# Two graph layers on one Trainium2 core: layer 1's early part over 17 blocks instead of 18, with five late lists, and a reordered tail

## Chip, core, metric

The kernel runs on one core of one Trainium2 chip. The metric is device time in microseconds (us). The kernel before has a median of 489.83 us over 9 runs (489.35 to 491.16).

Engines: TensorE (PE in the profile; PEld is its weight load), VectorE (DVE), ScalarE (ACT), GpSimd (POOL), SyncE (SP). Each works through its own queue strictly in the order in which the program recorded the instructions. SP issues plain DMAs; POOL issues the indirect ones (a gather or a scatter of 128 rows of 2 KB by a list of row numbers).

## What is computed

Cut to what matters, N = 2708 rows, D = 512, everything float32:

```python
# layer 0
d   = rowsum(adj) ** -0.5
x   = layernorm(x + relu((d[:,None] * adj * d[None,:]) @ x @ W + b))
# layer 1, 4 heads
xn     = x @ W_node + b_node
feats  = einsum('nd,hdf->hnf', xn, K)
logits = s[:, :, None] - 1e10 * (1 - adj)      # attn = softmax(logits)
x   = layernorm(x + relu(mean_h(attn @ feats)))
```

`adj` is sparse: about 0.3% of its entries are nonzero, with values between 0.05 and 1, and the diagonal is always there. The factor -1e10 makes the softmax a choice: each row takes the one column with the largest entry of `adj`. So layer 1 is `u = h @ M + c` for every row (`M` is `W_node` times the mean of the four `K`), then `y[row] = u[idx[row]]`, then `layernorm(h + relu(y))`. A flag sends the kernel into a dense path where this would not hold; with these inputs that path is not taken.

## The kernel before, in words

**Blocks and chunks.** The 2708 rows are 22 blocks of 128 (the last has 20). A search stage finds up to seven nonzeros in each third of a row. Then the main loop (line 1146) runs over `NS` = 21 blocks, and in each over nine chunks c = 0 to 8. A chunk is one gather of 128 rows of `v = d * (x @ W)` by POOL (L611) and one addition of it: c = 0, 3, 6 by DVE (L662), the other six by two-pass matmuls of PE (L672). POOL fetches up to 22 chunks ahead, but the last eight chunks of a block need that block's list, which DVE makes two blocks earlier (`hot`, `listed`).

**Layer 0's norm and h @ M.** At c = 8 `norm_1` adds the block up (L711, L712), and ACT squares it (L721). In the next block come `root_1` (ACT square root, L742; one DVE operation, L743), `root_2` (four small DVE operations, L748 to L751), `nbs` (L1186) and `norm_3` (ACT, L756), which gives the block's rows `h`. SP stores them to `h_d`. PE then turns them (`turn_h`, L224), ACT copies the turned tile to `sT` (L226), PE multiplies by `M` (`u_product`, L235), DVE adds `c` (`u_store`, L790), and the result `u` goes to DRAM.

**The 22nd part, L.** Up to 128 rows with too many nonzeros are listed and computed as a dense row product over the loop (`acc_l`, L1012, until block 17). They are normed (L1022, L1023, L761), turned and multiplied as one more block, `L`.

**Early and late.** `u` is kept in two DRAM tensors: `u_e` holds the rows of the first `EARLY` = 18 blocks, `u_d` the rest. Once blocks 0 to 17 and `L` are in `u_e`, the rows whose `idx` points into `u_e` can be finished: `y_fetch(n)` gathers `u_e` by `idx` for block n (L1052), `y_1` adds and squares (DVE L1063 and L720, ACT L721), `root_1` and `root_2` do three blocks together, `y_3` norms (ACT L756, or DVE L761 for each third block), and SP stores the block to the output. Rows whose `idx` points into `u_d` are the late ones: they were ranked beforehand into `NLATE` = 4 lists of 128 rows. After the last block, `late_h` gathers their `h`, `fetch_some` their `u`, and `put` (L1029) scatters the finished rows over the output. The rows of `L` are a fifth such list.

**What orders the work.** The order is written out by hand in the loop. `later(k, f)` issues f k chunks on. The pieces of layer 1 are the list `early_y`, from which `pieces_y(1)` takes one; `y_ahead(k)` issues the next k fetches. In the kernel before, `u_product` of block b runs in block b + 2 for the last blocks (at c = 1; block 17 at block 18, c = 8), the first puts into `u_e` follow at blocks 18 and 19, and the pieces start four chunks after the puts become possible, three in four chunks. Three blocks of `y_1` are done when the loop ends, and the other 18 follow.

Of the kernel before, what the change touches and what calls it, by code (L numbers as in the profile page):

```python
# [39 lines left out]
F32 = mybir.dt.float32  # L40
# [10 lines left out]
NEG = -10000000000.0  # L51
GAP = -200.0
CAP = 128
EARLY = 18
NLATE = 4
DIRECT = 1
ROOTS_AT = 10
BY_VECTOR = range(1, 21)
# [5 lines left out]
def tile_two_graph_layers(  # L64
# [552 lines left out]
    def row_space():  # L617

        ring[0] += 1
        if late is not None and ring[0] % 2:  # L620
            return late.tile([P, D], F32, name="g2", bufs=12)
        return g_pool.tile([P, D], F32, name="g", bufs=12)

    def fetch_chunk(ib, c):
# [157 lines left out]
    def u_store(ib):  # L782

        pr = P if ib == L else rows(ib)
        ut = dl["u"] if ib == L else pool2.tile([P, D], F32, name="ut", bufs=2)
        po, on_pe = products_u.pop(ib)
        if on_pe:
            nc.scalar.copy(ut[:pr], po[:pr])
        else:
            nc.vector.tensor_add(ut[:pr], po[:pr], c_bc[:pr])  # L790
        if ib < EARLY - 1:
            store(u_e, ut, ib)
        elif ib == EARLY - 1:
            later(1, lambda: put(ut, u_e[:, :], dl["own"][:, ib : ib + 1], EARLY * P))
        elif ib != L:
            late_put = lambda: put(ut, u_d[:, :], dl["own_d"][:, ib : ib + 1], N - EARLY * P)
            late_put() if ib >= NS - 2 else later(3, late_put)
        u_done.add(ib)


# [257 lines left out]
            oob_is_err=False,  # L1058
        )

    def y_1(n):
        t = h_of[n]
        nc.vector.scalar_tensor_tensor(t, ys[n], 0.0, t, op0=ALU.max, op1=ALU.add, accum_out=tot[:, n : n + 1])  # L1063
        squares(n, P, t, ys.pop(n))


    def y_3(n):
        (norm_3 if n % 3 else norm_v)(n, P, h_of[n])


    GROUP = 3
    n_pieces = NS + 13
    early_y = [[] for _ in range(n_pieces)]
    for n in range(NS):
        last = n // GROUP * GROUP + GROUP - 1
        early_y[n].append(lambda n=n: y_fetch(n))
        early_y[n + 6].append(lambda n=n: y_1(n))
        if n == last:
            early_y[last + 8].append(lambda n=n: root_1(n - GROUP + 1, n + 1))
            early_y[last + 9].append(lambda n=n: root_2(n - GROUP + 1, n + 1))  # L1080
        early_y[last + 10 + n % GROUP].append(lambda n=n: (y_3(n), store(out, h_of[n], n)))

    def pieces_y(k):
        for _ in range(k):
# [61 lines left out]
    for ib in range(NS):  # L1146
        pr = rows(ib)
        for c in range(C):
            n = ib * C + c
            form_until(n + 11)  # L1150
            fetch_until(n + (9 if n < 14 else 11) + (0 if found_at is None else min(11, max(0, 2 * (ib - found_at - 3)))))
            add_chunk(ib, c)
            group_of = max(g for g in GROUPS if g <= hot_next)
            if (
                c in (0, 5)
                and hot_next < NS
                and hot_next <= ib + (2 if c == 0 else 4)
                and group_of in starts
                and not (c == 5 and found_at is not None and ib == found_at + 1)
            ):  # L1160
                hot(hot_next)
                listing[n + 4] = lambda k=hot_next: enlist(k)
                listing[n + 6] = lambda k=hot_next: listed(k)
                hot_next += 1
            if n in listing:
                listing.pop(n)()
            if ib == 0 and c in (5, 8):
                weights(2 if c == 5 else 3)
            if finds and c in ((1, 4, 7) if ib < 3 else (1, 5)):
                search_next()  # L1170
            if c == 2 and not finds and found_at is None:
                group(GROUPS[2])
                searching[0] = False
                found_at = ib
            if found_at is not None:
                for f in plan.pop((ib - found_at, c), []):
                    f()
            if c == 2 and ib > ROOTS_AT:
                root_1(ib - 1, ib)
            if c == (2 if ib <= ROOTS_AT else 3) and ib:  # L1180
                k = slice(ib - 1, ib)
                if ib <= ROOTS_AT:
                    norm_2(ib - 1, ib, rows(ib - 1))
                else:
                    root_2(ib - 1, ib)
                    nc.scalar.activation(nbs[:, k], nms[:, k], AF.Copy, scale=rss[:, k])  # L1186
                norm_3(ib - 1, rows(ib - 1), space(ib - 1))
                store(h_d, space(ib - 1), ib - 1)
                waiting_h.append(ib - 1)
            if c == (7 if ib < EARLY else 6):  # L1190
                for _ in range(2):
                    if waiting_h:
                        turn_h(waiting_h.pop(0))
            for k in sorted(products_u):
                u_store(k)
            if c == (5 if ib < EARLY else 8 if ib == EARLY else 1) or (ib == EARLY and c == 5):
                for k in sorted(hTs):
                    u_product(k)
            if found_at == ib - 3 and c == 4:
                products_l = list(range(NB))  # L1200
            if c % 2 and products_l:
                listed_turn(products_l.pop(0))
            elif len(dl.get("turned", [])) > (2 if products_l else 0):
                listed_product(dl["turned"].pop(0))
            if dl.get("at") == n - 2:
                root_1(L, L + 1)
                root_2(L, L + 1)
                norm_v(L, P, h_of[L])
                waiting_h.append(L)
            if L in h_of and "at" not in dl:  # L1210
                dl["at"] = n
            if "set" not in dl and u_done >= set(range(EARLY - 1)) | {L}:
                dl["set"] = n
                later(3, lambda: put(dl["u"], u_e[:, :], dl["put"][:, NLATE:], EARLY * P))
                later(5, lambda: put(dl["u"], u_d[:, :], dl["put_d"], N - EARLY * P))
            if "go" not in dl and u_done >= set(range(EARLY)) | {L}:
                dl["go"] = n + 4
            if n >= dl.get("go", n + 1) and (n - dl["go"]) % 4 != 3 and n < len(chunks) - 3:
                pieces_y(1)
            tick()  # L1220
        if not finds and late is None:

# [18 lines left out]
    assert not due and not products_u  # L1241

    ib = NS - 1
    u_product(ib - 1)
    y_ahead(4)
    u_store(ib - 1)
    root_1(ib, ib + 1)
    root_2(ib, ib + 1)
    norm_v(ib, P, space(ib))
    store(h_d, space(ib), ib)  # L1250
    stir(16)
    turn_h(ib)
    u_product(ib)
    y_ahead(4)
    pieces_y(5)
    for k in range(NLATE):
        late_h(k)
    u_store(ib)
    ys[L] = row_space()
    fetch_some(ys[L], dl["top"][:, NLATE:], u_e[:, :], EARLY * P)  # L1260
    y_ahead(NS)

    order = [L + 1, L + 2, L] + list(range(L + 3, L + 1 + NLATE))
    for n in order:
# [8 lines left out]
        k = NLATE if n == L else n - L - 1  # L1273
        put(h_of[n], out_views[k], dl["put"][:, k : k + 1])

    pieces_y(16)
    bad1 = small.tile([P, 1], F32, name="bad1")
    nc.vector.tensor_reduce(bad1, bad, axis=AX.X, op=ALU.max)
    po = p_po.tile([P, D], F32, name="po")
    nc.tensor.matmul(po[:1, :1], bad1, ones, start=True, stop=True)  # L1280
    for n in first:
        y_1(n)
        pieces_y(1)
    root_1(min(first), max(first) + 1)
    for n in second:
        y_1(n)
        pieces_y(1)
        if n == second[0]:
            root_2(min(first), max(first) + 1)
            for k in first:  # L1290
                y_3(k)
    root_1(second[0], second[-1] + 1)
    pieces_y(n_pieces)
    for n in first:
        rows_out(n)
    root_2(second[0], second[-1] + 1)
    nc.vector.tensor_copy(bad_i, po[:1, :1])
    for n in second:
        y_3(n)
        rows_out(n)  # L1300
    main.close()
    in_order.close()
# [144 lines left out]
```

## Time and profile before

| | |
|---|---|
| median of 9 runs | 489.83 us |
| the profiled execution | 491.44 us |
| its span, first to last instruction | 489.7 us |
| mean granted TensorE clock | 0.917 of full |
| busy share of the span | DVE 80%, PE 77%, ACT 64%, POOL 62% |
| `norm_1` of block 15, 16, 17, 18, 19, 20 starts (DVE L711) | 366.31, 379.44, 395.96, 406.47, 416.12, 428.73 us |
| first and last fetch of `u_e` by `idx` (POOL L1052) | 420.24, 458.28 us |
| first and last gather of late `u` from `u_d` | 459.75, 465.03 us |
| last scatter to the output, its issue ends | 483.46 us |

The page of the profile gives sums over the whole span. The change touches only the last quarter, so it is read by the timeline of each engine (start, duration, engine, line, operation, and in brackets the idle time before it with what ended it) and by a table of windows (busy time of each engine in a stretch, with the granted clock PEclk and the DMA share).

### The profile page before, as it was taken

The page shows a single profiled execution, that of the slowest core. Times are in us where ns is not written, and L with a number is a line of the kernel's source. Part 1 is how long each engine was busy: PE and PEld are TensorE (multiplying, and loading weights), DVE is VectorE, ACT ScalarE, POOL GpSimd, SP SyncE. Part 2 cuts the span into 40 slices and gives each one's busy share as a digit, 9 for nine tenths or more (in the row PEclk, how much of TensorE's full clock was granted, in tenths as well). Part 3 has the DMA queues.
Part 4 walks back from the last instruction along what each step waited for, and adds up shares of the span by engine and source line. Part 5 has one row for each costly group of instructions (what it writes and reads, how often), then busy time and mean ns, then how long its engine had stood idle before and what let it go on. Part 6 is the DMA issues. An engine that isn't in the chain of part 4 may idle for free.

```text
span 489.7 us, 5318 instructions
## 1 busy us (share of the span) xinstructions
PE 375.6 (77%) x1129; PEld 168.4 (34%) x1129; DVE 392.9 (80%) x1079; ACT 312.5 (64%) x575; POOL 305.9 (62%) x434
## 2 busy tenths in 40 slices
PE   5968787667988989799878858799999999782000
PEld 3434343333223333344323423344444444340000
DVE  2899979899499999999999995766666797548761
ACT  2599999797986556776772454855566322337880
POOL 2343544453477577777777676777777565677703
PEclk9999999998997989999989979799999999977555
DMA  7999999998548678889888789999999687468952
GB/s 225 420 398 414 422 336 372 362 327 331 197 124 288 189 232 270 258 260 311 280 247 292 224 271 385 360 331 380 345 374 301 213 272 255 138 186 274 329 212 84
DMA packets 51565, 140.67 MB, mean 287 GB/s; under 512 B 10617, under 2 KB 10617, under 8 KB 48688
## 3 DMA queue, kind: packets, MB, share of 16 engines
q0 software_dynamic: 21840, 68.29, 44.9%
q1 hardware_dynamic: 29684, 71.95, 39.0%
q8 instruction: 11, 0.18, 0.2%
q14 instruction: 30, 0.25, 0.1%
HBM read 117.33 MB, written 24.99 MB: 291 GB/s over the span
## 4 chain that ended last, share of the span: by engine, by line
DVE 29%; PE 28%; DMA 21%; ACT 9%; issue 9%; POOL 1%; SPq 1%; POOLq 0%; DVEq 0%; ACTq 0%
PE acc L672 12%; DMA a<-in_adj_dram 12%; PE po L235 8%; DMA x<-in_x_dram 5%; DVE ats L319 5%; DVE vals L318 4%; PE acc_l L1012 4%; DVE hot L393 2%; DMA l_a<-in_adj_dram,to_read 2%; DVE vs L662 2%; ACT a L305 2%; ACT a L299 2%; PE tp L224 1%; PE po L504 1%; DVE past L392 1%
## 5 line engine op out<-in xcount | busy, mean ns | idle before, releaser
L611 POOL DMA_INDIRECT g<-v_d,l_col x126 | 127.8, 1014 | 43.3 <-issue 23.1
L672 PE MATMUL acc<-g,s 128*128 128x512 f32 x278 | 144.4, 634 | 3.9 <-DMA g<-v_d,l_col 2.6
L235 PE MATMUL po<-m_sb,sT 128*128 128x512 f32 x176 | 83.8, 622 | 4.0 <-ACT sT L226 4.0
L235 PE MATMUL acc<-w_sb,sT 128*128 128x512 f32 (+1 forms) x176 | 82.4, 613 | 0.0
L611 POOL DMA_INDIRECT g<-v_d,cols x63 | 62.8, 997 | 19.7 <-issue 11.6
L318 DVE MAX8 vals<-a 128x8 f32<-128x896 f32 (+2 forms) x66 | 71.7, 1086 | 2.0 <-ACT a L299 2.0
L319 DVE FIND_INDEX8 ats<-vals,a 128x8 uint32<-128x896 f32 (+2 forms) x66 | 72.0, 1091 | 0.0
L672 PEld LDWEIGHTS acc<-g,s 128*128 128x128 f32 x278 | 50.1, 200 | 50.3 <-issue 43.0
L305 ACT ACTIVATE a<-a 128x2708 f32<-128x2708 f32 (+1 forms) x22 | 54.1, 2460 | 13.6 <-DVE ats L319 13.6
L299 ACT ACTIVATE a<-a 128x2708 f32<-128x2708 f32 (+1 forms) x22 | 54.4, 2473 | 10.5 <-POOL a L311 10.5
L235 PEld LDWEIGHTS po<-m_sb,sT 128*128 128x128 f32 x176 | 34.5, 200 | 47.7 <-issue 39.8
L649 ACT ACTIVATE s<-s,l_val,l_minus 128x128 f32<-128x128 f32 x86 | 42.4, 493 | 2.9
L235 PEld LDWEIGHTS acc<-w_sb,sT 128*128 128x128 f32 (+1 forms) x176 | 32.4, 195 | 34.1 <-issue 34.0
L226 ACT COPY sT<-tp 128x512 f32<-128x512 f32 (+1 forms) x44 | 25.4, 577 | 28.3 <-PE tp L224 28.3
L311 POOL TENSOR_SCALAR_AFFINE_SELECT a<-a 128x128 f32<-128x128 f32 (+1 forms) x22 | 6.6, 299 | 57.2 <-DMA a<-in_adj_dram 52.0
L224 PE MATMUL tp<-ident,x 128*128 128x128 f32 (+1 forms) x88 | 15.0, 298 | 30.8 <-DMA x<-in_x_dram 21.6
L662 DVE SCALAR_TENSOR_TENSOR vs<-g,scaled,vs 128x512 f32<-128x512 f32 x50 | 37.3, 745 | 0.1
L648 ACT ACTIVATE s<-place,l_row 128x128 f32<-128x128 f32 x86 | 33.4, 388 | 0.0
L393 DVE SCALAR_TENSOR_TENSOR hot<-slots,ends,past 128x256 bf16<-128x256 bf16 x63 | 30.6, 485 | 2.2
L1052 POOL DMA_INDIRECT g<-u_e,idx x21 | 22.2, 1058 | 7.9 <-issue 5.5
L224 PEld LDWEIGHTS tp<-ident,x 128*128 128x128 f32 (+1 forms) x88 | 10.3, 151 | 42.7 <-issue 25.0
L726 ACT ACTIVATE nms<-tot 128x1 f32<-128x1 f32 x10 | 2.0, 202 | 35.1 <-DVE h_early L712 20.1
(265 smaller groups left out, 579.0 us busy)
## 6 DMA issues: line engine op xcount, KB each, us to landing
a<-in_adj_dram SPq DMA_DIRECT2D x21, 1354.0 KB, 9.5
x<-in_x_dram SPq DMA_DIRECT2D x21, 256.0 KB, 19.3
vs<-v_d SPq DMA_DIRECT2D x21, 256.0 KB, 4.8
xr<-in_x_dram SPq DMA_DIRECT2D x21, 256.0 KB, 5.8
l_v<-v_d SPq DMA_DIRECT2D x21, 256.0 KB, 5.9
u_e<-ut SPq DMA_DIRECT2D x17, 256.0 KB
h_d<-h_late SPq DMA_DIRECT2D x13, 256.0 KB, 2.8
out_dram<-h_late SPq DMA_DIRECT2D x13, 256.0 KB, 4.3
```

The lines of the kernel that those rows point to most:

```text
L224: nc.tensor.transpose(ps[:, f, :pr], src[:pr, f * P : (f + 1) * P], ident[:pr, :pr])
L235: nc.tensor.matmul(po[:pr], sT[:, f, :pr], wt[:, f, :], start=(f == 0 and row_3 is None), stop=(f == ND - 1))
L299: nc.scalar.activation(a, a, AF.Copy, accum_out=sums[:pr, ib : ib + 1])
L305: nc.scalar.activation(a, a, AF.Relu, scale=-1.0, accum_out=bad[:pr, NB + ib : NB + ib + 1])
L318: nc.vector.max(out=vals[:pr, ib, t, :], in_=part)
L319: nc.vector.max_index(out=ats[:pr, ib, t, :], in_max=vals[:pr, ib, t, :], in_values=part)
L393: nc.vector.scalar_tensor_tensor(h_t[:, t, :], slots, ends[:, 0, ib - lo, t : t + 1], past, op0=ALU.is_gt, op1=ALU.subtract)
L611: nc.gpsimd.indirect_dma_start(out=t[:pr], out_offset=None, in_=src, in_offset=bass.IndirectOffsetOnAxis(ap=ap, axis=0))
L648: nc.scalar.activation(s[:, :pr], place[:, :pr], AF.Abs, bias=minus_row[:, t : t + 1])
L649: nc.scalar.activation(s[:, :pr], s[:, :pr], AF.Relu, scale=minus_val[:, t : t + 1], bias=val[:, t : t + 1])
L662: nc.vector.scalar_tensor_tensor(vs, g, scaled[:, ib, CHUNKS[c][1], 0:1], vs, op0=ALU.mult, op1=ALU.add)
L672: nc.tensor.matmul(acc[ib][:pr], ss.pop((ib, c))[:k, :pr], g[:k], start=(first and not bias_on_pe(ib)), stop=(c == len(CHUNKS) - 1),)
```

## The change

- `EARLY` is 17 and `NLATE` is 5. So `u_e` is complete one block sooner, one more list of late rows is gathered, fetched and put, and the lists' ranking on DVE has one more step per list.
- From block 16 on, `root_1` is at c = 1, `root_2` and `norm_3` at c = 2, `turn_h` at c = 5 and `u_product` at c = 3 or 7 of the **next** block: `u` of block b is made in block b + 1. The products of 14 and 15 are both in block 16, those of 16 and `L` in block 17, and 17, 18 and 19 in blocks 18, 19 and 20.
- The puts into `u_e` follow the products by one and two chunks, and from three chunks on one `y_fetch` is issued per chunk. In POOL's queue the three puts and the first fetch now stand ahead of the nine gathers of block 20, and two more fetches stand among these.
- From seven chunks after that point on, a piece of layer 1 is taken at c = 2, 5 and 8: additions 0 to 6 are in the loop (0 in block 18; 1, 2, 3 in 19; 4, 5, 6 in 20).
- `root_1` and `root_2` of layer 1 go over groups of 5, 5, 5, 3 and 3 blocks; all norms but two are ACT's.
- Row buffers: 12, 9 and 4 in a cycle of seven instead of 12 and 12.
- After the loop: fewer transposes that do nothing but keep PE busy (`stir`), the fetches are all issued, the norm of block 20 comes after one piece, and the late lists are done three and three.

```diff
-EARLY = 18
-NLATE = 4
+EARLY = 17
+NLATE = 5
...
-        if late is not None and ring[0] % 2:
-            return late.tile([P, D], F32, name="g2", bufs=12)
+        if late is not None and ring[0] % 7 % 2:
+            return late.tile([P, D], F32, name="g2", bufs=9)
+        if late is not None and ring[0] % 7 == 6:
+            return late.tile([P, D], F32, name="g3", bufs=4)
...
-            late_put() if ib >= NS - 2 else later(3, late_put)
+            late_put() if ib >= NS - 1 else later(1, late_put)
...
+    ENDS = [5, 10, 15, 18, NS]
+    early_y = [[] for _ in range(NS + 16)]
+    lo = 0
+    for hi in ENDS:
+        for n in range(lo, hi):
+            early_y[n].append(lambda n=n: (y_add(n), y_square(n)))
+        early_y[hi].append(lambda lo=lo, hi=hi: root_1(lo, hi))
+        early_y[hi + 1].append(lambda lo=lo, hi=hi: root_2(lo, hi))
+        for n in range(lo, hi):
+            out_n = lambda n=n: (y_3(n, n > 13 and n % 3 == 0), store(out, h_of[n], n))
+            early_y[hi + 2 + (n - lo)].append(out_n)
+        lo = hi
...
-            if c == 2 and ib > ROOTS_AT:
+            if c == (2 if ib < EARLY - 1 else 1) and ib > ROOTS_AT:
                 root_1(ib - 1, ib)
-            if c == (2 if ib <= ROOTS_AT else 3) and ib:
+            if c == (3 if ROOTS_AT < ib < EARLY - 1 else 2) and ib:
...
-            if c == (7 if ib < EARLY else 6):
+            if c == (7 if ib < EARLY - 1 else 5):
...
-            if c == (5 if ib < EARLY else 8 if ib == EARLY else 1) or (ib == EARLY and c == 5):
+            if c == 5 and ib < EARLY - 1 or ib >= EARLY - 1 and c in (3, 7):
                 for k in sorted(hTs):
                     u_product(k)
...
-                later(3, lambda: put(dl["u"], u_e[:, :], dl["put"][:, NLATE:], EARLY * P))
-                later(5, lambda: put(dl["u"], u_d[:, :], dl["put_d"], N - EARLY * P))
+                later(1, lambda: put(dl["u"], u_e[:, :], dl["put"][:, NLATE:], EARLY * P))
+                later(2, lambda: put(dl["u"], u_d[:, :], dl["put_d"], N - EARLY * P))
...
-                dl["go"] = n + 4
-            if n >= dl.get("go", n + 1) and (n - dl["go"]) % 4 != 3 and n < len(chunks) - 3:
-                pieces_y(1)
+                dl["go"] = n + 3
+            if n >= dl.get("go", n + 1):
+                y_ahead(1)
+                if n >= dl["go"] + 4 and c % 3 == 2:
+                    pieces_y(1)
...
-    u_product(ib - 1)
-    y_ahead(4)
-    u_store(ib - 1)
     root_1(ib, ib + 1)
+    pieces_y(1)
     root_2(ib, ib + 1)
     norm_v(ib, P, space(ib))
     store(h_d, space(ib), ib)
-    stir(16)
+    stir(12)
     turn_h(ib)
+    y_ahead(NS)
+    pieces_y(2)
     u_product(ib)
-    y_ahead(4)
-    pieces_y(5)
+    pieces_y(2)
     for k in range(NLATE):
         late_h(k)
-    u_store(ib)
...
+    u_store(ib)
```

More of the change, by code (lines that the diff above doesn't have):

```diff
@@ L1059, in fetch_some, with y_add, y_square, y_3 @@
         )
-    def y_1(n):
+    def y_add(n):
         t = h_of[n]
         nc.vector.scalar_tensor_tensor(t, ys[n], 0.0, t, op0=ALU.max, op1=ALU.add, accum_out=tot[:, n : n + 1])
[L1064 to L1081, printed above, removed]
+        nc.vector.tensor_scalar(nms[:, n : n + 1], tot[:, n : n + 1], -1.0 / D, None, op0=ALU.mult)
+    def y_square(n):
+        k = slice(n, n + 1)
+        nc.scalar.activation(ys.pop(n), h_of[n], AF.Square, bias=nms[:, k], accum_out=sqs[:, k])
+    def y_3(n, by_vector=False):
+        (norm_v if by_vector else norm_3)(n, P, h_of[n])
+    ENDS = [5, 10, 15, 18, NS]
[10 more added lines that the diff above has]
+        lo = hi
     def pieces_y(k):
@@ L1250, in tile_two_graph_layers @@
     store(h_d, space(ib), ib)
-    stir(16)
+    stir(12)
     turn_h(ib)
+    y_ahead(NS)
+    pieces_y(2)
     u_product(ib)
-    y_ahead(4)
-    pieces_y(5)
+    pieces_y(2)
     for k in range(NLATE):
         late_h(k)
-    u_store(ib)
     ys[L] = row_space()
     fetch_some(ys[L], dl["top"][:, NLATE:], u_e[:, :], EARLY * P)
-    y_ahead(NS)
+    u_store(ib)
     order = [L + 1, L + 2, L] + list(range(L + 3, L + 1 + NLATE))
@@ L1274, in rows_out @@
         put(h_of[n], out_views[k], dl["put"][:, k : k + 1])
-    pieces_y(16)
+    pieces_y(NS + 16)
     bad1 = small.tile([P, 1], F32, name="bad1")
@@ L1281, in tile_two_graph_layers @@
     for n in first:
-        y_1(n)
-        pieces_y(1)
+        y_add(n)
+        y_square(n)
     root_1(min(first), max(first) + 1)
     for n in second:
-        y_1(n)
-        pieces_y(1)
+        y_add(n)
+        y_square(n)
         if n == second[0]:
@@ L1291, in tile_two_graph_layers @@
                 y_3(k)
-    root_1(second[0], second[-1] + 1)
-    pieces_y(n_pieces)
     for n in first:
         rows_out(n)
+    root_1(second[0], second[-1] + 1)
+    nc.vector.tensor_scalar(bad_i, po[:1, :1], 0.0, None, op0=ALU.is_gt)
     root_2(second[0], second[-1] + 1)
-    nc.vector.tensor_copy(bad_i, po[:1, :1])
     for n in second:
-        y_3(n)
+        y_3(n, n == second[1])
         rows_out(n)
```

## The prediction

> **What bounds the kernel now.** I read the table of windows first, cut at the starts of `norm_1` of blocks 17 to 20 and at the tail's turning points.
>
> ```profile
> core 0: us, PE busy (x) PEld busy (x) DVE busy (x) ACT busy (x) POOL busy (x), PEclk, DMA share, GB/s
> 396.00:406.50 10.50, 10.50 (x29) 4.91 (x28) 9.02 (x31) 2.80 (x6) 6.90 (x7) 1.00 0.85 261
> 406.50:416.10 9.60, 9.19 (x25) 4.10 (x24) 7.02 (x20) 2.80 (x6) 4.10 (x5) 1.00 0.76 266
> 416.10:428.70 12.60, 9.23 (x24) 3.75 (x23) 7.49 (x22) 4.55 (x11) 8.62 (x9) 1.00 0.46 137
> 428.70:438.10 9.40, 8.52 (x24) 4.38 (x24) 3.36 (x12) 1.69 (x6) 7.26 (x8) 0.64 0.62 177
> 438.10:469.00 30.90, 4.33 (x12) 1.86 (x12) 23.60 (x105) 24.25 (x56) 21.83 (x21) 0.62 0.90 301
> ```
>
> Until 416 PE is full: it sets the pace. In block 20 nothing is full; the blocks' end waits for early pieces. Then 9.4 us pass in which PE is busy at a clock of 0.64. From 438 to 469 ACT and DVE alternate (24 of 31 us each), three blocks of layer 1 per 4.8 us. POOL's timeline comes second, since its queue holds gathers, puts and fetches in one order:
>
> ```profile
> 400.27 0.95 POOL L611 DMA_INDIRECT g<-v_d,l_col  x1 [1.83 <-DVE l_val L438]
> ...
> 410.79 1.02 POOL L1029 DMA_INDIRECT u_e<-l_u,to_put  x1 [0.30 <-DVE ut L790]
> 416.10 0.99 POOL L1029 DMA_INDIRECT u_e<-ut,put_own  x1 [4.29 <-DMA h_d<-h_late]
> 417.40 0.99 POOL L1029 DMA_INDIRECT u_d<-l_u,put_d  x1 [0.30 <-issue]
> 420.24 1.05 POOL L1052 DMA_INDIRECT g<-u_e,idx  x1 [1.84 <-DMA u_e<-ut,put_own]
> ...
> 465.03 1.00 POOL L1052 DMA_INDIRECT g<-u_d,top_d  x1 [0.30 <-issue]
> ```
>
> The second put starts 5.3 us after the first into the same tensor, the first fetch 4.1 us after the second put. (The named h_d store is the latest event; the put before it fits.) After that POOL issues 34 instructions in 44.8 us, 1.36 us each, without a gap, so it ends just before the late additions (469.0) need it. Third, ACT's timeline, for the chain of layer 0's norm:
>
> ```profile
> 408.12 0.72 ACT L721 ACTIVATE xr<-h_late,nms 128x512 f32<-128x512 f32 x1 [2.78 <-DVE nms L720]
> 408.74 0.19 ACT L721 ACTIVATION_READ_ACCUMULATOR xr<-h_late,nms 128x1 f32 x1
> 408.96 0.29 ACT L742 ACTIVATE sds<-sqs,eps 128x1 f32<-128x1 f32 x1
> 412.51 0.29 ACT L1186 ACTIVATE nbs<-nms,rss 128x1 f32<-128x1 f32 x1 [3.26 <-DVE rss L751]
> 412.84 0.81 ACT L756 ACTIVATE h_late<-h_late,nbs,rss 128x512 f32<-128x512 f32 x1
> ```
>
> Block 18 starts its `norm_1` at 406.47 and its `h` is ready at 413.65. Before, this delay is hidden: the product follows most of a block later, and PE has the next block's chunks meanwhile.
>
> **The change, part by part.** Times are the trace's, A(b) is the start of `norm_1` (L711) of block b.
>
> *Ranking.* One more L897 (0.20) and L904 (0.12), and L910 a fifth longer (0.74 to 0.87): 0.45 us on DVE at 276 to 278, where DVE has no idle time until 297. I take **+0.4**; nothing if the gather queue hides it.
>
> *Blocks 16 and 17.* Both hold one product (3.43 us) more or earlier: 14 and 15 in 16, 16 and `L` in 17. PE was full in 16, so A(16) is 3.4 later (382.7), and so is the end of `acc_l` (386.3 for 382.2 + 1.1). From there the chain of `L` (two DVE operations, square, root, norm) gives its `h` at 393.2. PE has lost its filler, the product of 15, and idles 2.5 us (389.0 to 391.5, for `h` of 16) and 1.25 us (to 393.25). Then chunk, two products, chunk: A(17) is **402.85**, for 395.96. 6.9 us of that are the two products, which block 18 no longer has.
>
> *Blocks 18 to 20.* Now the whole chain lies in one block: L711, L712, sum (1.6 us); square and square root (to 2.9); DVE's four operations (3.7); `nbs` and `norm_3` (4.85); turn and one chunk (6.2); four matmul pairs of the product (9.65); then, ahead of the next L711 on DVE, `u_store` (0.62), a piece's addition (0.86) and the own term (0.66): **11.8 us**. In block 18 the list of block 20 stands before `root_2`: 1.55 less 0.3 of slack, 13.1. In block 20 `root_2` over five replaces the own term: 12.15. PE's own work is 9.0 us per block. So A(18) = 415.95, A(19) = 427.75, A(20) = **439.9**, for 428.73: 11.2 later. The old loop left product 19 outside, though, and that cost it the 9.4 us at low clock.
>
> *POOL.* Block 19's list is 2.4 later (behind L1022/L1023), so its gathers end near 400. First put 400, second 405, third 406.3, first fetch 409.1 instead of 420.24. The nine gathers of block 20 are queued behind them, from 410.5 to 423; block 20 needs them from 428 on, so nothing waits. But fetches 1 to 3 are issued at 419.2, 421.75 and 424.35; a landing takes 3.3 to 4.1 (420.24 to its use at 423.54, 422.96 to 427.07), so addition 3 can start at 427.9, and without other delay A(19) is 429.4, **+1.65**. Till the last late gather come 45 more instructions and one exposed put (4.2): it starts near 472 (465.03 before), lands at 476, and by the tail's steps the span would end at 489.6. POOL alone therefore gives no gain: the ten-microsecond earlier start is spent on nine gathers, a put, a list and its late gather.
>
> *Tail.* From A(20), ACT: square and root 2.8, piece, `h` of 20 at 4.85, its turned copy to 6.1. Then 18 norms and 13 squares back to back at 0.71 and 0.72 (before: 448.95 to 450.6), four roots, some 2 us where DVE's root of a group stands between two additions, 1.3 for product 20 (PE idle 4.7 us before it, so at half clock): late additions from A(20) + 31.4 (before +40.3). Three late blocks, the next three, the last put issued at +46 (before +54.7: 483.46 less 428.73). The 6.2 us behind the last put (483.46 to 489.7) stay. The span ends at A(20) + **52.15**.
>
> *PE's clock.* New idle times are 2.5 and 1.25 (block 17), 3.15 (18), 2.6 and 2.6 (19, 20). What an idle time does to the matmuls behind it, from PE's timeline:
>
> ```profile
> 172.97 1.12 PE L224 MATMUL tp<-ident,h_early 128*128 128x128 f32 x4 [2.73 <-ACT h_early L756]
> 173.88 1.92 PE L672 MATMUL acc<-g,s 128*128 128x512 f32 x2
> ...
> 200.86 0.66 PE L224 MATMUL tp<-ident,h_early 128*128 128x128 f32 x4 [2.51 <-ACT h_early L756]
> 201.35 1.02 PE L672 MATMUL acc<-g,s 128*128 128x512 f32 x2
> ...
> 429.34 6.77 PE L235 MATMUL po<-m_sb,sT 128*128 128x512 f32 x8 [3.31 <-ACT sT L226]
> ```
>
> A pair takes 1.92 for 1.02, a product 6.77 for 3.60. Of seven idle times from 2.5 to 3.0, three (2.73, 2.85, 2.96) were followed by half speed; all longer ones were. A drop costs about 1.7 (111.9: 1.5, 148.5: 1.9, 255.2: 1.6), 3.3 at most (429.3). I take about half of 1.7 (0.85) for blocks 17, 19 and 20 and all of it for 18: **+4.25**, between 0 and 13. These delays come ahead of addition 3, so the 1.65 is then no wait any more. The Trainium skill ("TensorE: Matmul & The Clock Gate", "HAM oscillation — how this bites in real kernels") speaks for the low end: only idle gaps over about 3.4 us should throttle. By it the 4.25 would be 0 and the sum 494 us; the rows at 2.73 to 2.96 say otherwise, and I follow them.
>
> **The sum.** 439.9 + 0.4 + 4.25 + 52.15 = 496.7 us of span, 7.0 more than 489.7. The profiled execution took 491.44 (1.74 around its span), the median is 489.83; I add 7.0 to the median: **496.8 us**, 1.4% slower.
>
> **Rivals.**
>
> 1. *The clock holds.* As for the sum, but no drop; then addition 3 is waited for: 439.9 + 0.4 + 1.65 + 52.15 = 494.1, median 494.2. For it: 2.51 and 2.79 us without a drop. Against: 3.15 in block 18.
> 2. *Faster: the chain hides.* If blocks 18 to 20 keep the old pace of 10.5, 9.65 and 9.65 us (406.47 to 416.12), A(20) is 433.05 and the tail ends at 485.6. The place is the step from L711 to the turned `h`; it decides where the three blocks take under 34.3 us (489.7 less 52.15, 402.85 and 0.4) instead of 37. But then POOL's queue ends the kernel at up to 489.6, less 2.4 if block 19's list is not late and 0.9 if a put lands in 4.1 instead of 5: 486.3. I price it 488. For it: PE's work is 9.0. Against: PE's order, where turn, chunk, product, chunk stand behind each other.
> 3. *The clock drops in all four blocks*, and each time for as long as at 429.3: 13.2 instead of 4.25, 505.7; with 1.7 each 499.3. I price it 502.5.
> 4. *The change does not do what it says*: `u_e` complete no sooner. The product of 16 and `L` would then end where 17's did (409.9) and POOL start at 420 again, with 12 more instructions at 1.36: 504. Instruction order speaks against it; I count it into 3.
>
> **Chances.** Forecast (495.5 to 499.3) 0.47; clock holds (492.4 to 495.5) 0.21; chain hides (486 to 491) 0.18; rival 3 and 4 (499.3 to 506) 0.14. Differences under 0.2% (488.85 to 490.81) can't be told from no change. Rival 2 gives 0.12 faster and 0.06 same, rival 1 0.02 same; so faster 0.12, same 0.08, slower 0.80. The range leaves out rival 2's lower part and rival 3's upper part, a tenth each: 489 to 502.
>
> **What would show it.** Right: L711 of block 17 near 403 and 11 to 13 us between the next ones; PE idle before each `tp` of `h_late` 2.5 us or more; first `u_e` fetch near 409 to 411, gathers of block 20 behind it; late additions some 31 us after A(20). Wrong: PE full in blocks 18 to 20, or DVE sitting at L1063 waiting for fetches by many microseconds, or an ACT tail with gaps.

## The result, and the profile after

The changed kernel takes 500.98 us (median of 10 runs, 498.82 to 503.63), the kernel before 489.82 in the runs beside it (31 runs, 486.02 to 492.49): a ratio of 1.0226, 95% interval 1.0203 to 1.0248. The profiled execution has a span of 501.0 us and a mean granted clock of 0.891 (before 489.7 and 0.917). The forecast was 496.8 us, slower, in a range of 489 to 502.

In the changed kernel a line L stands 2 further down (`norm_1` is L713, `norm_3` L758, `u_store` L792, additions L1065, fetches L1054, puts L1031); `nbs` is L1191. The table of windows, cut at the starts of `norm_1` of blocks 17 to 20 and at the first late addition (columns as in the header line):

```profile
core 0: us, PE busy (x) PEld busy (x) DVE busy (x) ACT busy (x) POOL busy (x), PEclk, DMA share, GB/s
406.04:421.14 15.10, 12.03 (x28) 5.50 (x27) 9.18 (x33) 3.35 (x7) 10.91 (x12) 0.89 0.64 196
421.14:434.71 13.57, 10.90 (x25) 4.89 (x24) 9.43 (x31) 5.14 (x13) 10.52 (x11) 0.87 0.75 234
434.71:448.48 13.77, 10.97 (x34) 5.29 (x32) 8.13 (x29) 4.79 (x13) 10.72 (x11) 0.88 0.60 180
448.48:479.47 30.99, 7.30 (x12) 3.00 (x12) 19.00 (x81) 26.42 (x56) 18.30 (x17) 0.64 0.77 248
```

Blocks 18 to 20 took 10.5, 9.65 and 12.6 us before and take 15.1, 13.6 and 13.8 now, at a clock of 0.87 to 0.89 instead of 1.00. PE was full in block 18 before and is full in none of them now. The way from A(20) to the first late addition has gone from 40.3 to 31.0 us. So A(20), the start of `norm_1` of block 20, is 19.75 us later (448.48 for 428.73): 1.1 of them stand at A(15) already, 9.0 come in blocks 16 and 17, which hold a product more, and 9.7 in blocks 18 to 20. The tail, A(20) to the end, gives 8.5 back (52.5 for 61.0). POOL's timeline:

```profile
402.31 1.03 POOL L1031 DMA_INDIRECT u_e<-ut,put_own  x1 [0.71 <-DVE ut L792]
406.07 0.99 POOL L1031 DMA_INDIRECT u_e<-l_u,to_put  x1 [2.73 <-DVE l_u L792]
...
409.47 1.05 POOL L1054 DMA_INDIRECT g<-u_e,idx  x1 [1.12 <-DMA u_e<-l_u,to_put]
410.82 0.99 POOL L611 DMA_INDIRECT g<-v_d,cols  x1 [0.31 <-DVE vrs L751]
...
465.41 1.02 POOL L1031 DMA_INDIRECT u_d<-ut,own_d  x1 [0.31 <-issue]
471.12 1.03 POOL L1054 DMA_INDIRECT g<-u_d,top_d  x1 [4.69 <-DMA u_d<-ut,own_d]
...
477.72 1.00 POOL L1054 DMA_INDIRECT g<-u_d,top_d  x1 [0.30 <-issue]
```

The first fetch starts 10.8 us sooner (409.47 for 420.24), the last late gather 12.7 later. ACT's timeline shows the chain of block 17's norm, now followed at once by its use:

```profile
407.68 0.72 ACT L723 ACTIVATE xr<-h_late,nms 128x512 f32<-128x512 f32 x1 [11.75 <-DVE nms L722]
...
408.52 0.30 ACT L744 ACTIVATE sds<-sqs,eps 128x1 f32<-128x1 f32 x1
411.13 0.29 ACT L1191 ACTIVATE nbs<-nms,rss 128x1 f32<-128x1 f32 x1 [2.31 <-DVE rss L753]
411.46 0.81 ACT L758 ACTIVATE h_late<-h_late,nbs,rss 128x512 f32<-128x512 f32 x1
413.35 0.59 ACT L226 COPY sT<-tp 128x512 f32<-128x512 f32 x1 [1.08 <-PE tp L224]
```

And PE's timeline shows what waits for it (the first four lines are block 17, then come 18, 19 and 20):

```profile
393.01 0.66 PE L224 MATMUL tp<-ident,h_late 128*128 128x128 f32 x4 [2.43 <-ACT h_late L758]
394.68 0.63 PE L224 MATMUL tp<-ident,l_h 128*128 128x128 f32 x4 [1.02 <-DVE l_h L763]
395.14 1.61 PE L674 MATMUL acc<-g,s 128*128 128x512 f32 x2
396.55 8.18 PE L235 MATMUL po<-m_sb,sT 128*128 128x512 f32 x16
...
412.33 0.98 PE L224 MATMUL tp<-ident,h_late 128*128 128x128 f32 x4 [3.07 <-ACT h_late L758]
413.11 1.91 PE L674 MATMUL acc<-g,s 128*128 128x512 f32 x2
414.82 4.15 PE L235 MATMUL po<-m_sb,sT 128*128 128x512 f32 x8
...
425.93 0.94 PE L224 MATMUL tp<-ident,h_late 128*128 128x128 f32 x4 [2.67 <-ACT h_late L758]
426.66 1.92 PE L674 MATMUL acc<-g,s 128*128 128x512 f32 x2
428.37 4.20 PE L235 MATMUL po<-m_sb,sT 128*128 128x512 f32 x8
...
439.50 0.86 PE L224 MATMUL tp<-ident,h_late 128*128 128x128 f32 x4 [2.63 <-ACT h_late L758]
440.15 1.92 PE L674 MATMUL acc<-g,s 128*128 128x512 f32 x2
441.86 4.28 PE L235 MATMUL po<-m_sb,sT 128*128 128x512 f32 x8
```

In blocks 18 to 20 each idle time ahead of a turn is followed by a pair that takes 1.91 or 1.92 instead of 1.02 us and a product of 4.15 to 4.28 instead of 3.60; in block 17 the pair takes 1.61 and the two products 8.18 (7.03 with the clock at 1.00, in the run with the filler of 20).

The last four kernels below (marked *) ran where every execution was disturbed: the kernel before took 537.99 us there (17 runs, 530.16 to 543.78), and engines in their traces stand still where nothing is named that they wait for (once for 9.95 us), so these four are compared with it there alone, and their ratios, which leave the more disturbed runs out, can differ from the quotient of the medians.

### The profile page after: what moved, and what is told of

It is laid out like the page before. It is cut to its first block, busy times and chain, and to the rows that moved or that the text cites. A ratio compares the mean times of both kernels' runs of the same rounds, so it can differ in the third digit from the quotient of the medians.

```text
span 501.0 us, 5295 instructions
## 1 busy us (share of the span) xinstructions
PE 390.3 (78%) x1125; PEld 174.2 (35%) x1125; DVE 391.0 (78%) x1066; ACT 318.3 (64%) x582; POOL 312.7 (62%) x438
## 4 chain that ended last, share of the span: by engine, by line
DVE 27%; PE 26%; ACT 6%; issue 4%; DMA 2%; POOL 1%; POOLq 0%; DVEq 0%
PE po L235 10%; PE acc L674 9%; PE acc_l L1014 4%; DVE ats L319 3%; DVE vals L318 2%; DVE hot L393 2%; DVE vs L664 2%; DMA l_a<-in_adj_dram,to_read 2%; PE tp L224 2%; DVE vs L713 2%; ACT h_late L758 2%; ACT g L1070 1%; DVE past L392 1%; DVE h_early L714 1%; DVE h_late L1065 1%
## 5 line engine op out<-in xcount | busy, mean ns | idle before, releaser
L674 PE MATMUL acc<-g,s 128*128 128x512 f32 x278 | 152.0, 661 | 3.6 <-DMA g<-v_d,l_col 1.8
L611 POOL DMA_INDIRECT g<-v_d,l_col x126 | 126.5, 1004 | 44.3 <-issue 26.9
L235 PE MATMUL po<-m_sb,sT 128*128 128x512 f32 x176 | 88.4, 650 | 0.7 <-ACT sT L226 0.7
L235 PE MATMUL acc<-w_sb,sT 128*128 128x512 f32 (+1 forms) x176 | 85.9, 635 | 0.0
L611 POOL DMA_INDIRECT g<-v_d,cols x63 | 66.2, 1051 | 19.9 <-issue 13.7
L674 PEld LDWEIGHTS acc<-g,s 128*128 128x128 f32 x278 | 51.6, 206 | 51.7 <-issue 42.6
L299 ACT ACTIVATE a<-a 128x2708 f32<-128x2708 f32 (+1 forms) x22 | 54.5, 2476 | 10.7 <-POOL a L311 10.7
L235 PEld LDWEIGHTS po<-m_sb,sT 128*128 128x128 f32 x176 | 37.3, 215 | 50.2 <-issue 44.6
L235 PEld LDWEIGHTS acc<-w_sb,sT 128*128 128x128 f32 (+1 forms) x176 | 33.8, 203 | 36.3 <-issue 36.2
L792 DVE TENSOR_TENSOR ut<-po,c_bc 128x512 f32<-128x512 f32 x15 | 10.3, 689 | 30.7 <-PE po L235 30.7
L1054 POOL DMA_INDIRECT g<-u_e,idx x21 | 22.8, 1088 | 7.2 <-issue 5.8
L723 ACT ACTIVATE xr<-h_late,nms 128x512 f32<-128x512 f32 x11 | 7.9, 722 | 28.8 <-DVE nms L722 28.8
## 6 DMA issues: line engine op xcount, KB each, us to landing
x<-in_x_dram SPq DMA_DIRECT2D x21, 256.0 KB, 12.6
```

The costliest lines, as they stand in the source:

```text
L235: nc.tensor.matmul(po[:pr], sT[:, f, :pr], wt[:, f, :], start=(f == 0 and row_3 is None), stop=(f == ND - 1))
L299: nc.scalar.activation(a, a, AF.Copy, accum_out=sums[:pr, ib : ib + 1])
L611: nc.gpsimd.indirect_dma_start(out=t[:pr], out_offset=None, in_=src, in_offset=bass.IndirectOffsetOnAxis(ap=ap, axis=0))
L674: nc.tensor.matmul(acc[ib][:pr], ss.pop((ib, c))[:k, :pr], g[:k], start=(first and not bias_on_pe(ib)), stop=(c == len(CHUNKS) - 1),)
```

## The experiments

My theory after the result: the loss is the chain of norm, turn and product inside one block, and the clock that drops in it. The rivals: POOL's order, and the fifth list with the pieces in the loop. The kernels, each with its ratio to runs of the kernel before taken beside it, and with A(20) and the tail (A(20) to the end of the span) of its profile:

| kernel | ratio to before, 95% | A(20) | tail |
|---|---|---|---|
| before | 1 | 428.73 | 61.0 |
| changed | 1.0226 (1.0203 to 1.0248) | 448.48 | 52.5 |
| changed, old places of h @ M | 1.0092 (1.0056 to 1.0128) | 442.66 | 52.1 |
| the same, additions one block later | 1.0164 (1.0135 to 1.0193) | 433.77 | 60.9 |
| before, new places only | 1.0080 (1.0050 to 1.0110) | 437.84 | 57.2 |
| before, 17 blocks and five lists only | 1.0074 (1.0048 to 1.0101) | 441.00 | 51.6 |
| changed, filler of 40 | 1.0204 (1.0167 to 1.0240) | 447.01 | 52.7 |
| changed, filler of 20 | 1.0264 (1.0233 to 1.0296) | 447.81 | 52.8 |
| changed, no additions in the loop | 1.0335 (1.0298 to 1.0371) | 440.63 | 62.2 |
| new tail, 18 blocks, four lists, old places, no additions in the loop | 1.0015 (0.9994 to 1.0037) | 426.30 | 62.6 |
| changed, additions one block later * | 1.0184 (1.0092 to 1.0277) | | |
| the same, filler of 20 * | 1.0210 (1.0109 to 1.0311) | | |
| changed, 18 blocks and four lists * | 1.0089 (1.0033 to 1.0146) | | |
| new tail, put ahead of five fetches * | none | | |

**The old places in the changed kernel.** Cut to the main lines:

```diff
...
-            if c == (2 if ib < EARLY - 1 else 1) and ib > ROOTS_AT:
+            if c == 2 and ib > ROOTS_AT:
...
-            if c == (7 if ib < EARLY - 1 else 5):
+            if c == (7 if ib < EARLY else 6):
...
-            if c == 5 and ib < EARLY - 1 or ib >= EARLY - 1 and c in (3, 7):
+            if c == (5 if ib < EARLY else 8 if ib == EARLY else 1) or (ib == EARLY and c == 5):
...
-    stir(12)
+    u_product(ib - 1)
+    u_store(ib - 1)
     turn_h(ib)
```

> The changed kernel with only the places of h @ M put back where they were (root of a block in chunks 2 and 3 of the next, turn in chunk 7 or 6, product in chunk 5, 8 or 1 of the block after); product 19 stands in the tail again, ahead of the turn of block 20, where it takes the place of the 12 filler transposes. Seventeen early blocks, five lists, the fetches, the additions in the loop and the new tail stay. My theory (the chain sum, root, norm, turn, product inside one block is the loss, 52 us of tail are not): blocks 18 to 20 return to some 9.7 to 10.5 us, norm_1 of block 20 starts near 430, plus 52.5 of tail and up to 2 for product 19: 484 to 490 us. Rival POOL order, and rival five lists / additions in the loop / tail: their cost stays, 497 to 501 us.

495.92 us, between the two expectations and outside both. Block 18 took 24.9 us. DVE's timeline of this kernel shows why:

```profile
419.11 0.69 DVE L1065 SCALAR_TENSOR_TENSOR h_early<-g,h_early 128x512 f32<-128x512 f32 x1 [13.36 <-DMA g<-u_e,idx]
```

and POOL's, where the fetch was:

```profile
406.65 0.99 POOL L611 DMA_INDIRECT g<-v_d,cols  x1 [0.30 <-issue]
...
414.24 0.95 POOL L611 DMA_INDIRECT g<-v_d,cols  x1 [0.30 <-DMA g<-v_d,cols]
415.49 1.02 POOL L1054 DMA_INDIRECT g<-u_e,idx  x1 [0.30 <-issue]
```

Seven gathers of later blocks stand ahead of the first fetch, and the addition that needs it stands ahead of `norm_1` of block 18 on DVE. So the rival "POOL's order" has its place too, only not in the changed kernel's own run.

**The same with the additions one block later.**

```diff
-                if n >= dl["go"] + 4 and c % 3 == 2:
+                if n >= dl["go"] + 13 and c % 3 == 2:
```

> The changed kernel with the old places of h @ M, as in the earlier run, and the first early addition in the loop one block later (chunk 8 of block 19 instead of block 18), since that run's VectorE waited 13.36 us for the first fetch, which stood in GpSimd's queue behind the gathers of blocks 19 and 20. Theory (that wait is what kept the old places from paying): norm_1 of block 20 near 432, tail 52: 484 to 487 us. Rival (GpSimd's queue ends the kernel anyway, its last late gather was issued at 474.42 and can come only some 2 us sooner): 490 to 493 us.

497.09 us, above both expectations. The loop did what I had hoped: A(20) is 433.77. But the tail is 60.9. DVE's timeline in the tail, the store of product 20:

```profile
448.39 0.69 DVE L792 TENSOR_TENSOR ut<-po,c_bc 128x512 f32<-128x512 f32 x1 [4.87 <-DMA u_d<-ut,own_d]
```

and POOL's:

```profile
444.50 1.02 POOL L1031 DMA_INDIRECT u_d<-ut,own_d  x1 [0.31 <-issue]
...
459.80 1.01 POOL L1031 DMA_INDIRECT u_d<-ut,own_d  x1 [0.30 <-DVE rss L750]
466.68 1.22 POOL L1054 DMA_INDIRECT g<-u_d,top_d  x1 [5.87 <-DMA u_d<-ut,own_d]
...
473.92 1.00 POOL L1054 DMA_INDIRECT g<-u_d,top_d  x1 [0.30 <-issue]
```

`ut` has two buffers, so product 20 waits for an earlier put of late rows, which stood in POOL's queue behind the fetches. DVE stands for 4.87 us and ACT behind it for 3.61; POOL, which issues without a gap from 405 to 460, issues its last late gather at 473.92, and the additions that need these gathers wait three times more, 0.2 to 0.5 us each. So waits that go back to POOL's queue are some 4.7 of the 8.4 us by which this tail is longer than the changed kernel's (3.61 on ACT, 1.07 on DVE). The rest is not taken apart: three squares more in the tail, about 0.72 us each, and product 19 stand in it.

**The new places alone, in the kernel before.** The edit is the mirror image of the first one, without the filler and the new tail.

> The kernel before with only the places of h @ M moved (from block 17 on, since its early part has 18 blocks); four lists, the old fetches, pieces and tail stay, only product 19 is no longer in the tail. My theory: blocks 18 to 20 take 13 us and more, with PE idle 2.5 us before each turn and half speed behind it; norm_1 of block 20 near 438 instead of 428.7, the tail loses 9.4 us of product 19: 490 to 497 us, within -0.1 to +1.5% of before. Rival (the loss is in the lists, the additions or the tail): no loss from the places, so the 9.4 us of product 19 are gained in part: 482 to 488 us.

495.37 us, as the theory said, though not in its parts: blocks 18, 19 and 20 take 14.3, 11.1 and 12.6 us, only the first with half speed, while block 17, which now holds two products, takes 20.8 for 16.5; and the tail gives back 3.8 us, not 9.4. PE's timeline:

```profile
406.09 0.66 PE L224 MATMUL tp<-ident,h_late 128*128 128x128 f32 x4 [3.03 <-ACT h_late L756]
406.58 1.02 PE L672 MATMUL acc<-g,s 128*128 128x512 f32 x2
407.44 5.37 PE L235 MATMUL po<-m_sb,sT 128*128 128x512 f32 x8
...
418.93 0.66 PE L224 MATMUL tp<-ident,h_late 128*128 128x128 f32 x4 [1.82 <-ACT h_late L756]
419.42 1.02 PE L672 MATMUL acc<-g,s 128*128 128x512 f32 x2
420.28 3.68 PE L235 MATMUL po<-m_sb,sT 128*128 128x512 f32 x8
```

After 3.03 us of idling the clock drops, here only with the product, and after 1.82 it does not. In block 19 of this kernel no addition stands in the chain, and the idle time is 0.85 us shorter than in the changed kernel (1.82 for 2.67).

**17 blocks and five lists alone, in the kernel before.** `EARLY = 17`, `NLATE = 5`.

> The kernel before with only 17 early blocks and five lists; the formula for the places of h @ M is unchanged (its bounds go by the number of early blocks), as are pieces and tail. My theory: the fifth list costs one more late block (about 1.6 us of ACT and DVE in the tail and 2.7 of POOL), and the earlier fetches give back up to 5 us that block 20 waited for them: 486 to 492 us. Rival (the fifth list and the queue of POOL are the loss): 495 to 501 us.

493.79 us, between the two. In this kernel the additions wait 5.43, 1.94 and 0.49 us in block 19 for fetches that stand behind eight gathers, and the product behind them runs at half speed (6.16 us): block 19 takes 20.7 us. So POOL's order costs here too; the fifth list's own work is not told apart from it.

**Is it the clock?** Transposes of the identity fill the time in which PE waits.

```diff
             if c == (7 if ib < EARLY - 1 else 5):
+                if ib >= EARLY:
+                    stir(40)
```

> The changed kernel with 40 extra transposes of the identity ahead of the turn of h in blocks 17 to 20, so that PE does not idle while it waits for norm_3; the chain itself is as long as before. My theory (7.0 us of the loss are half-speed matmuls behind an idle PE): the turn, the pair and the product take 0.6, 1.02 and 3.6 us again, blocks 18 to 20 take some 12 to 13 us instead of 13.6 to 15.1, 494 to 496 us. Rival (latency of the chain alone, the clock does no harm): 500 to 502 us. If the filler holds the turn up, above 501.

501.27 us, no gain, though the granted clock is 1.00 in blocks 17 to 20. This is the expectation's third case: 40 transposes took 4.53 us, too long: the copy to `sT` waited 1.5 to 2.3 us for the turn behind them in three of the four blocks. With 20:

> The changed kernel with 20 filler transposes (2.27 us, by 4.53 us for 40 in the run with the long filler) ahead of the turn of h in blocks 17 to 20, so that they end before h is ready (PE idles 2.4 to 3.1 us there). Theory clock: matmuls at full speed without a later turn, blocks 18 to 20 take 12 to 13 us, but early additions may wait 1 to 2 us for their fetches once: 494 to 497 us. Rival (the chain's latency alone counts, what the clock costs is hidden by the waits for fetches): 500 to 502 us.

502.56 us, outside the theory's 494 to 497, and the profile tells why nothing was gained. The windows of blocks 18, 19 and 20:

```profile
403.70:417.10 13.40, 12.54 (x48) 6.77 (x47) 9.17 (x33) 3.35 (x7) 8.45 (x8) 1.00 0.55 156
417.10:435.57 18.47, 14.19 (x46) 7.21 (x45) 9.38 (x31) 5.13 (x13) 14.51 (x14) 0.82 0.69 220
435.57:447.81 12.24, 11.58 (x54) 6.77 (x52) 8.21 (x30) 4.79 (x13) 9.50 (x10) 1.00 0.58 179
```

Blocks 18 and 20 are 1.70 and 1.53 us shorter than in the changed kernel, at a clock of 1.00, and block 17 is 1.70 shorter (20.06 for 21.76). Block 19 is 4.90 longer. PE's timeline in it:

```profile
421.89 0.66 PE L224 MATMUL tp<-ident,h_late 128*128 128x128 f32 x4 [0.42 <-ACT h_late L758]
422.38 1.02 PE L674 MATMUL acc<-g,s 128*128 128x512 f32 x2
427.28 6.19 PE L235 MATMUL po<-m_sb,sT 128*128 128x512 f32 x8 [3.87 <-ACT sT L226]
```

ACT's:

```profile
425.94 0.72 ACT L1070 ACTIVATE g<-h_early,nms 128x512 f32<-128x512 f32 x1 [4.10 <-DVE nms L1066]
...
426.66 0.56 ACT L226 COPY sT<-tp 128x512 f32<-128x512 f32 x1
```

and DVE's:

```profile
425.02 0.69 DVE L1065 SCALAR_TENSOR_TENSOR h_early<-g,h_early 128x512 f32<-128x512 f32 x1 [4.35 <-DMA g<-u_e,idx]
```

Addition 1 reaches DVE 4.35 us before its rows land; its square stands ahead of the copy to `sT` in ACT's queue, the product waits for the copy, and the 3.87 us of PE's idling bring the half speed back. 1.70 + 1.70 + 1.53 less 4.90 is nothing. In the changed kernel the same fetch is issued at 419.64 for 419.95, but the slow clock has delayed DVE, so that the addition starts at 424.62 and does not wait. Two limits stand close together, and taking one away shows the other.

**Additions out of the loop.** `dl["go"] + 99` in the condition above, so that all come in the tail.

> The changed kernel with no early addition inside the loop: all of them come in the tail. Theory (the additions cost 0.86 us of DVE ahead of norm_1 in each of blocks 18 to 20, and save 0.72 us of ACT each in the tail): norm_1 of block 20 is 2.6 us earlier, the tail is up to 6 times 0.72 = 4.3 us longer: 501 to 503 us. Rival (the additions and their waits are the main loss): A(20) falls by 5 us and more, 495 to 498 us.

505.11 us, above both expectations. Blocks 19 and 20 fall to 11.1 and 10.7 us, at a clock of 1.00 (idle times 1.87 and 1.81). The tail grows by 9.7, more than the 4.3 of ACT's squares: DVE's store of product 20 waits 3.42 us for PE, the sixth addition stands behind it, and ACT idles 3.63 us for that one. Neither theory's sum held; the additions in the loop are worth more than they cost there.

**The additions later, without and with the short filler \*.**

> The changed kernel with the early additions of the loop from chunk 8 of block 19 on instead of block 18 (four instead of seven), so that none waits for its fetch. It is the partner of the next run, which adds the filler. Theory: block 18 and 19 are 2 to 3 us shorter together, the tail 2 to 5 us longer (without any addition in the loop it was 9.7 longer): 500 to 503 us, with PE idle 1.8 to 3 us ahead of the turns and half speed behind some of them.

> The same with the short filler of 20 transposes ahead of the turn in blocks 17 to 20. Theory (half speed costs 1.5 to 2 us wherever no wait for a fetch covers it): 2 to 5 us less than its partner without the filler. Rival (the clock costs nothing, the chain sets the pace): within 1 us of its partner.

Ratios 1.0184 (1.0092 to 1.0277) and 1.0210 (1.0109 to 1.0311): the intervals cover each other, so the 2 to 5 us that the filler was to bring do not show, and the pair decides nothing about the whole time (block 20 of the profile with the filler stood for 29.8 us). Block 18, where no addition stands in either, takes 14.26 us without and 12.60 with the filler, the 1.7 us seen above.

**18 blocks and four lists in the changed kernel \*.** `EARLY = 18`, `NLATE = 4`.

> The changed kernel with 18 early blocks and four lists, as before the change; places of h @ M (one block later, from block 17 on, since they go by the number of early blocks), one fetch per chunk, additions and tail as changed. Theory (places and lists each cost, and most of it adds up: places alone gave +0.8%, 17 blocks with five lists alone +0.7%): 493 to 497 us. Rival (the fifth list is the greater part in this tail): 489 to 491 us; rival (places and tail are all): 499 to 501 us.

Median 538.01 us beside 537.99, ratio 1.0089 (1.0033 to 1.0146). The ratio fits places at 0.8% with the tail at +0.15% (below); the medians show no difference. So this run supports the sum but does not carry it.

**The new tail alone.** The kernel with old places and later additions, with 18 blocks and four lists. It was meant to keep one addition in the loop, but keeps none: the first starts at 428.87, behind `norm_1` of block 20. The kernel before has three in the loop, so the tail is not quite alone.

> The kernel just described with 18 early blocks and four lists again, and one early addition in the loop only (chunk 8 of block 20): the kernel before with the new tail, product 19 behind the norm of block 20. Theory (the places and the lists are the loss, the tail is a gain): norm_1 of block 20 at 426 to 429, no wait of 9.4 us for product 19, so 52 to 55 us of tail: 480 to 486 us, faster than the kernel before. Rival (GpSimd's queue or ScalarE's additions end it as before): 488 to 491 us.

490.99 us for 489.79: no difference. A(20) is the soonest of all (426.30), product 19 costs nothing any more, and still the tail is 62.6. DVE's timeline:

```profile
469.52 0.69 DVE L1065 SCALAR_TENSOR_TENSOR g<-g,g 128x512 f32<-128x512 f32 x1 [4.03 <-DMA g<-u_d,top_d]
471.26 0.69 DVE L1065 SCALAR_TENSOR_TENSOR g<-g 128x512 f32<-128x512 f32 x1 [0.85 <-DMA g<-u_d,top_d]
```

POOL's:

```profile
458.56 1.02 POOL L1031 DMA_INDIRECT u_d<-ut,own_d  x1 [0.30 <-DVE rss L750]
464.93 1.02 POOL L1054 DMA_INDIRECT g<-u_d,top_d  x1 [5.35 <-issue]
```

DVE waits for the late gathers, and these for the put of block 20, which the new order puts behind all fetches, so that 5.35 us of its landing are exposed (the profile names nothing for this wait; in two other kernels it names the put, and the next run agrees); the kernel before has five other fetches there. I tried the put ahead of five fetches:

```diff
-    y_ahead(NS)
+    y_ahead(1)
     pieces_y(2)
     u_product(ib)
     pieces_y(2)
+    u_store(ib)
+    y_ahead(NS)
...
-    u_store(ib)
```

> The run with the new tail (18 early blocks, four lists, old places) showed ScalarE done with the early blocks at 466.4 and the late additions held until 469.5 and 471.3 by the fetches behind the put of block 20, for whose landing GpSimd waited 5.35 us. Here that put is issued as soon as product 20 is stored, ahead of four early fetches, the gathers of late h and one fetch more (9 instructions, 12 us), so that its landing is hidden. Theory: the last late gather is issued near 465 instead of 470, ScalarE ends the early blocks as before, late additions from 466.5: 4 to 5 us less, 485 to 487 us, faster than the kernel before by 0.6 to 1%. Rival (the late additions wait for something else, or the early fetches that now come after the put hold ScalarE up): 489 to 491 us.

This is a kernel marked *: 529.07 us (six runs, 516.72 to 534.78) beside 537.99 of the kernel before. The wait did go: the first late gather is issued 0.30 us behind the instruction before it, the last one 13 us ahead of the additions, which wait for nothing. But in its profile the late additions come 51.8 us after A(20), and the six runs scatter by 3.4%, too much for a ratio with an interval, so whether this version beats the kernel before stays open. No other version had a ratio under 1.

## Why the prediction was right, and where it was not

The span is 4.3 us over the sum (501.0 for 496.7): A(20) 3.9 later than the 444.55 that the sum gives it, the tail 0.4 longer. The range held, with 1 us to spare; the forecast's own stretch (495.5 to 499.3, chance 0.47) did not. 500.98 lies in the stretch of rivals 3 and 4, which had 0.14, and the sign of 11 to 13 us between the next `norm_1` did not come (15.1, 13.6, 13.8). So the direction and most parts were right, one term was not, and that the range held owes something to its width.

- *Ranking, +0.4.* A(15) is 1.1 us later. But over the profiles of the kernels with five lists A(15) goes from 364.6 to 367.4, for 366.3 before: the term in A(15) is smaller than what one execution can show. In DVE's queue it is there: the ranking ends 0.51 us later, from a start 0.07 later.
- *Blocks 16 and 17.* Block 16 takes 16.87 us for 16.4, and 16.87 to 16.90 in the other three kernels with these places and five lists, so this 0.5 was mis-sized. Block 17 without the clock (filler of 20): 20.06 for 20.15.
- *The chain.* Right: with the clock held, 13.40 for 13.1 in block 18 and 12.24 for 12.15 in block 20. For the 11.8 of block 19 no run shows it without a wait for a fetch.
- *PE's clock, +4.25.* **This step failed, by its size.** I took half of 1.7 where three of seven idle times in the trace were followed by half speed; that is a mean over two cases, not the likelier one. I also left out of the count two shorter idle times close together in the trace before (2.30 and 2.37 us, ahead of 306.38 and 309.94), behind which a turn takes 1.11 and a pair 1.92; block 17 has such two (2.43 and 1.02). All four blocks dropped; they exceed the chain by 1.6, 2.0, 1.8 and 1.6, together 7.0, and the filler takes 1.70, 1.70 and 1.53 of it away in blocks 17, 18 and 20, where no fetch is waited for; for block 19 the share of the clock is not shown. The Trainium skill's rule ("TensorE: Matmul & The Clock Gate", "HAM oscillation — how this bites in real kernels": no idle gap over about 3.4 us) would have made this term 0; these runs contradict it as a bound, with drops behind 2.63, 2.67 and 3.07 us.
- *POOL.* The first fetch at 409.47 was forecast at 409.1. The last late gather near 472 came at 477.72: 2.98 us are idle time ahead of the gathers of late `h` (457.02), which the forecast did not have (that it is the later A(20) is argued, not shown), 0.5 the longer wait for the put, 0.4 the start, and the rest lies in the issues. In the changed kernel it holds almost nothing up, as forecast: one addition waits 0.65 us, and DVE starts the late additions at 479.47 without a wait.
- *Tail, 52.15.* 52.5, late additions at A(20) + 31.0 for 31.4.
- *Rival 1, the clock holds (494.2).* The filler of 20 set its condition in blocks 17, 18 and 20, and the time was 502.56. I had looked for the wait at addition 3 (1.65 us); it comes at addition 1 (4.35), and goes on over ACT's queue into the product, a road that I had not followed. My own numbers had the wait: fetch 1, issued at 419.2, lands at 422.5 at the soonest, and addition 1 stands 3.5 us behind A(18), so near 419.9 by this rival.
- *Rival 2, the chain hides (488).* The old places with later additions set it nearly to the point: A(20) is 433.77 for 433.05. The span was 494.7, 5.1 over the 489.6 at which I had POOL's queue end the kernel: the last late gather is issued at 473.92 for 472, and from there to the end it takes 20.8 us, not 17.6. This kernel has product 19 in its tail, which the rival had not, so it is no clean test; but no ratio here lies on the faster side of my range.
- *Rival 3, the clock drops in all four blocks.* This is what happened, at the 1.7 us of its lower price (499.3).
- *Rival 4.* `u_e` was complete sooner, as the change says.

What of the 2.26% is whose? Places alone cost 0.80%, 17 blocks with five lists 0.74%, the tail 0.15%: 1.7% of 2.26%. The tail's number includes three additions fewer in the loop. The rest, 0.6%, is less than the half-widths of the four intervals together (1.0%), so I do not explain it. My first theory, that the places were the whole loss, fell with the first run: each part alone costs, and undoing one uncovers a fetch or a put in POOL's queue.

## What to carry to other kernels

A product that is moved nearer to the norm that feeds it loses its cover: count the whole chain into the block, and the filler that PE loses. Where several engines' limits lie within some us of each other, a wait that vanishes is not a gain until the next one is priced, along each queue that the waiting instruction stands in (here addition, its square, the copy behind it, the product). And when half speed follows idle times of a size in some cases, price it at all of them or none, and keep both sums; half of each is the price of neither.

## What the runs showed of the hardware

- In the last blocks half speed followed PE's idle times of 2.43 and 1.02 us close together, 2.63, 2.67, 3.03, 3.07 and 3.17 us, and none of 1.80 to 1.87 (four); in the kernel with five lists alone it followed one of 1.99 (granted clock 0.64 in the 4 us from there). In kernels marked * it followed 3.10 twice and did not follow 2.97. With those of the kernel before (2.50 to 2.86 without, 2.73 to 2.96 with) that is no single limit.
- Nor does the length decide at one place of the program: the idle time of 2.86 us ahead of an early turn was followed by a product of 3.60 us in the kernel before (92.78) and of 4.57 in the changed one (92.23), and that of 2.51 near 200 us by a pair of 1.02 before and of 1.91 with the filler of 20. What decides is open.
- The drop can come about 1.4 us after the idle time's end (new places only: a pair at 1.02 us, then the product at 5.37).
- 20 or 40 transposes of the identity (0.11 us each) in the idle time kept the granted clock at 1.00, 40 in blocks 17 to 20, 20 in 17, 18 and 20. The Trainium skill ("TensorE: Matmul & The Clock Gate", "Part 4: PE-mode transpose") says that in transpose mode a transpose does not count as PE's business in the same way; the trace lists these as matmuls and does not show the mode, but they did hold the clock.
- In these kernels a gather from a tensor just put to stood on POOL until the put had landed: 4.69 us in the changed kernel, 5.87 and 6.07 in two others, where the profile names the put, and 5.35 in one where it names nothing; POOL's queue stands meanwhile.
- A fetch of 128 rows landed 5.1 us after its issue (419.95 to 425.02), where the kernel before had shown 3.3 to 4.1.
